# Score-factor broadcasts of the first pair by TensorE, setup weights in small tiles, and a finer order model, in a four-layer graph network

## The chip, the cores and the metric

The kernel runs on one core of a Trainium2 chip. The metric is the device time of the whole kernel in microseconds, the median of several executions. One further execution was taken under the hardware profiler; what is read from the profile comes from that one.

## The reference

There are 64 graphs of 256 nodes with 256 features, each with a 0/1 adjacency matrix of which about one entry in 64 is set. Four layers follow one another, each on the layer-normalised, rectified input, and each added to the running x:

```python
h = jnp.maximum(_layernorm(x, axis=-1), 0.0)
x = x + _L0_gnn_ref(h, adj, L0_gnn_W, L0_gnn_a_src, L0_gnn_a_dst)        # 4 heads of 64, slope 0.2, elu
h = jnp.maximum(_layernorm(x, axis=-1), 0.0)
x = x + _L1_gnn_ref(h, adj, L1_gnn_W, ...)                               # 4 heads of 64, slope 0.01, relu, residual, layer norm per head
h = jnp.maximum(_layernorm(x, axis=-1), 0.0)
x = x + _L2_gnn_ref(h, adj, L2_gnn_W, L2_gnn_a)                          # 1 head of 256, slope 0.2
h = jnp.maximum(_layernorm(x, axis=-1), 0.0)
x = x + _L3_gnn_ref(h, adj, L3_gnn_weight, L3_gnn_w_ih, ...)             # 3 rounds: adjacency sum, then a GRU cell
```

Layers 0 to 2 are graph attention. The score of an edge from i to j is a leaky ReLU of s_i + d_j, where s and d are products of the projected features with two vectors; a softmax over the neighbours weighs the projected features. In layer 3 a round is `m = h @ weight[i]`, `aggr = A^T m`, and a GRU cell with gates r, z and n on `aggr` and `h`.

## The kernel before, in words

The graphs go in 32 pairs. A pair's nodes are 4 blocks of 128 rows (C = 4), so its features are a tile `xt` of 128 x 4 x 256.

**An attention layer** (`heads_of`, or `layer2`). `norm` takes statistics on VectorE (L962, L963), the power -1/2 on GpSimd (L971, L972), and ScalarE writes the normalised, rectified `xn` (L980). `transposed` turns it by TensorE (L997) and ScalarE copies the banks into `ht`. `project` multiplies with the weights (L1019), in whose extra two columns per head stand the weights of s and d; ScalarE copies the result into `wh` (L1032, L1034). `factors` makes what the softmax needs. Since exp of a leaky ReLU of a sum is the larger of two products, each edge's weight is, up to a factor that the softmax divides out, the larger of f[0] and f[1] * cb, where `f` has one value per row j and head (L1072), and `cb` holds for every i the value exp((slope-1) * s_i), the same in all 128 partitions. To get `cb`, TensorE transposes the column of s to a row (L1053), ScalarE takes the exponential (L1060), ScalarE's DMA queue writes the row to memory (`rd`, L1065), and SP's queue reads it back for all partitions (`cb<-rd`, L1066; 1 MB for four heads, 256 KB for one). Then, for each head, `weights` makes `pt` by four VectorE instructions (L1087) and takes the minimum with `cap`, the mask made of the adjacency; `attend_head` multiplies `pt` with `wh` on TensorE (L1107), and VectorE divides by the sum.

**The mask.** SP loads the adjacency into the one `at` slot; ScalarE squares it (L1150, a check of the values), VectorE sums its rows (L1156), GpSimd casts it (`am`) and makes `cap_n` (L1164); TensorE turns that (L1177) and ScalarE copies it into `cap`.

**The GRU** (`gru`). Per round, TensorE does two aggregations (L1304), twelve gate groups (L1318; four 128-row products each with `ht`,`whh` or with `ag`,`wc`) and two row transposes (L1332); ScalarE takes the tanh, GpSimd one subtraction, and VectorE the rest.

**Setup.** The vectors of the scores are broadcast by ScalarE's queue into `ag` and `o` tiles; `score_column` multiplies them with the weights, reduces and copies the result into the weights' extra columns, all on VectorE. `input_gates` multiplies the three GRU weights with `w_ih` to `wc` (L925), from two tiles in the two `cb4_` slots, which are the same slots that hold a layer's `cb`.

**The order.** Nothing runs in the order in which it is written. Each `op(...)` only records an operation with its engine, a cost in nanoseconds, what it reads, writes and takes. `_Schedule.run` then plays all of them through once, at build time: an operation's due time follows backwards from the end of its pair, an engine that is idle takes the operation with the earliest due time whose inputs are done and whose buffers are free, and the instructions are emitted in that order. On each engine they run strictly in it. Buffers are slots of fixed number (`cb4_` 2, `at` 1, `pt` 3, `g` 9, `bank` 8, `xt` 5, and others), so a transfer also waits until its slot's last reader is done. All loads, broadcasts and stores but the small ones go through SP's queue, in order. Most VectorE, ScalarE and GpSimd instructions are issued by one helper, and so have one line, L807.

Of the kernel before, what the change touches and what calls it, by code (L numbers as in the profile page):

```python
# [517 lines left out]
SLOPES = (0.2, 0.01, 0.2)  # L518

# [18 lines left out]
class _Schedule:  # L538
# [8 lines left out]
    HOP = 300  # L547
    DMA_LATENCY = 2000
    DMA_RATE = 250.0
    STRETCH = 3.0  # L550

# [67 lines left out]

    def run(self):  # L620
        ops = self.ops
        for o in reversed(ops):
            late = self.end[o.group]
            for s in o.succs:
                if s.group == o.group or o.group not in self.end or o.group < 0:
                    late = min(late, s.due - self.STRETCH * s.cost - self.HOP)
            if o.nbytes:
                late -= self.DMA_LATENCY + o.nbytes / self.DMA_RATE
            o.due = late
# [17 lines left out]
        while True:  # L647
            for e in engines:
                if not idle[e]:
                    continue  # L650
                held = []
                while able[e]:
# [6 lines left out]
                    if all(len(self.free[c]) >= n for c, n in need.items()):  # L659
# [9 lines left out]
                        post(clock + o.cost, "free", o)  # L669
# [7 lines left out]
            while events and events[0][0] == clock:  # L677
                _, _, kind, o = heapq.heappop(events)
                if kind == "free":
                    idle[o.engine] = True  # L680
                    t = clock
                    if o.nbytes:
                        self.dma_free = max(self.dma_free, clock) + o.nbytes / self.DMA_RATE
                        t = self.dma_free + self.DMA_LATENCY
                        post(t, "done", o)
                    else:
                        post(t + self.HOP, "done", o)
                        for s in o.succs:
                            if s.engine == o.engine:
                                s.waits -= 1  # L690
                                if s.waits == 0:
                                    heapq.heappush(able[s.engine], (s.due, s.index))
                elif kind == "done":
                    done += 1
                    for s in o.succs:
                        if o.nbytes or s.engine != o.engine:
                            s.waits -= 1
                            if s.waits == 0:
                                heapq.heappush(able[s.engine], (s.due, s.index))
# [9 lines left out]
def _fast_path(  # L709
# [105 lines left out]
    def dma(engine, nbytes, emit, reads=(), writes=(), takes=()):  # L815
        op(engine, 450 if engine == "sp" else 120, emit, reads, writes, takes, nbytes)
# [4 lines left out]
    w3, wih = buf("cb4_", [P, L, DC, D]), buf("cb4_", [P, DC, G])  # L821
# [33 lines left out]
    for i in range(L):  # L855
        dma("sp", 1 << 18, lambda i=i: nc.sync.dma_start(
            w3.tile[:, i], w3t[i].rearrange("(c p) d -> p c d", p=P)), (), [(w3, i)])
    dma("sp", 3 << 18, lambda: nc.sync.dma_start(
        wih.tile, wih_t.rearrange("(c p) g -> p c g", p=P)), (), [wih])
# [4 lines left out]
    def score_column(B_we, w_ap, vec_buf, v_ap, dst, k, dc, s):  # L864
# [3 lines left out]
        vec(nc.vector.tensor_mul, 330, view, w_ap, v_ap,  # L868
            reads=[(B_we, (dc, "w")), vec_buf], writes=[tmp])
        col = lambda: cols.tile[:, dc, k : k + heads]  # L870
        vec(nc.vector.tensor_reduce, 330, col, view, AX.X, OP.add, reads=[tmp], writes=[(cols, (dc, k))])
        vec(nc.vector.tensor_copy, 80, dst, col, reads=[(cols, (dc, k))], writes=[(B_we, (dc, s))])
# [47 lines left out]
    def input_gates(i, dc, g0, g1):  # L920
        ps = bank()

        def mm():
            for ec in range(DC):
                nc.tensor.matmul(  # L925
                    ps.tile[:, : g1 - g0],
                    lhsT=w3.tile[:, i, ec, dc * P : (dc + 1) * P],
                    rhs=wih.tile[:, ec, g0:g1],
# [4 lines left out]
        op("pe", (g1 - g0) * 3.4, mm, [(w3, i), wih], [ps])  # L933
        vec(nc.scalar.copy, 150 + (g1 - g0), wc[:, i, dc, g0:g1], lambda: ps.tile[:, : g1 - g0],
            reads=[ps], writes=[(B_wc, (i, dc, g0))], engine="act")

    for i in range(L):
        for dc in range(DC):
            for g0 in (0, 512):
                input_gates(i, dc, g0, min(g0 + 512, G))  # L940
# [8 lines left out]
    op("dve", 300, gate_biases, [bi, bh], [B_bg])  # L949
# [5 lines left out]
    def norm(xt, cls):  # L955
# [19 lines left out]
        vec(nc.vector.scalar_tensor_tensor, 120, lambda: mv.tile[:, 3, :], lambda: mv.tile[:, 0, :], -1.0,  # L975
# [13 lines left out]
    def transposed(xn, cls):  # L989
        ht = buf(cls, [P, DC, S])  # L990

        def block(dc):
# [8 lines left out]
            op("pe", 470, emit, [xn], [ps], takes=[ht])  # L1001
# [7 lines left out]
    def project(ht, we, B_we, heads, width, shift):  # L1009
# [4 lines left out]
        def rows(c):  # L1014
# [12 lines left out]
            op("pe", 910, emit, [ht, B_we], [ps], takes=[wh])  # L1027
# [14 lines left out]
    def factors(wh, heads, width, slope, shift):  # L1042
# [6 lines left out]
        ps, row, rd = bank(), buf("row", [R, P]), buf("rd", [R, P])  # L1049
        cb = buf(f"cb{heads}_", [P, heads, C, P])  # L1050

        def emit_t():
            nc.tensor.transpose(  # L1053
                ps.tile[:R, :P], wh.tile.rearrange("p h c w -> p (h c) w")[:, :, width + 1], ident
            )

        op("pe", 150, emit_t, [wh], [ps])

        def emit_row():
            nc.scalar.activation(  # L1060
                row.tile, ps.tile[:R, :P], AF.Exp, scale=slope - 1.0, bias=-shift * (slope - 1.0)
            )

        op("act", 260, emit_row, [ps], [row])
        dma("act", 1 << 13, lambda: nc.scalar.dma_start(rd.tile, row.tile), [row], [rd])  # L1065
        dma("sp", heads << 18, lambda: nc.sync.dma_start(  # L1066
            cb.tile.rearrange("p h c n -> p (h c n)"),
            rd.tile.rearrange("(o r) n -> o (r n)", o=1).to_broadcast([P, R * P]),
        ), [rd], [cb])

        def exps(k, a):
            op("act", 250, lambda: nc.scalar.activation(  # L1072
# [8 lines left out]
    def weights(cap, f, cb, h):  # L1081
# [11 lines left out]
        for b in range(2):  # L1093
            for jc in range(2):
                op("dve", 440, lambda b=b, jc=jc: emit(b, jc), [cb, f], [(pt, (b, jc))])
# [16 lines left out]
    def attend_head(o, o_view, pt, wh, h):  # L1112
# [7 lines left out]
        op("pe", 980, emit, [pt, wh], [ps], takes=[o])  # L1120
        rs = buf("rs", [P, C])
        view = lambda: ps.tile[:, : C * w].rearrange("p (c w) -> p c w", c=C)
        vec(nc.vector.reciprocal, 190, lambda: rs.tile, lambda: view()[:, :, E], reads=[ps], writes=[rs])
# [344 lines left out]
```

## Time and profile before

| | |
|---|---|
| median of 3 runs | 3286.79 us (3286.14 to 3287.27) |
| profiled execution | 3288.5 us, its span 3286.6 us |
| TensorE busy | 3184.5 us, 97% of the span |
| VectorE | 2368.8 us, 72% |
| ScalarE | 1453.9 us, 44% |
| GpSimd | 1103.6 us, 34% |
| moved by DMA | 134.02 MB, 41 GB/s |

In the profile's lines PE is TensorE (PEld its weight loads), DVE is VectorE, ACT is ScalarE, POOL is GpSimd and SP is SyncE; DVEq, ACTq and SPq are the engines' queues. A line names the source line, the engine, the operation, the output and input by the program's names, the tile shapes and how many instructions. In a timeline the first two numbers are the start and the length in us, and a bracket at the end gives the idle time before the instruction and what ended it. PEclk is the granted TensorE clock in tenths of full speed.

### The profile page before, as it was taken

Reading aid. Unit: us, or ns where it says so; the run is one execution under the profiler, and the core shown is the slowest. Engines: PE = TensorE matmul, PEld = TensorE weight load, DVE = VectorE, ACT = ScalarE, POOL = GpSimd, SP = SyncE. Lnnn points to the kernel's source line nnn. Section 1 sums busy time; section 2 is a strip of 40 time slices with the busy share of each in tenths; the row PEclk is TensorE's granted clock in tenths of the full one; section 3 lists DMA queues with packets and bytes.
Section 4 is the critical chain, followed back from the end, with each engine's and each line's share of the span. In section 5 each row is a group of like instructions: output and inputs, shape, how many; then the busy total and the mean of one; then the engine's idle time right before and its main releaser. Section 6 shows DMA issues by size and latency. Waiting matters only on the chain.

```text
span 3286.6 us, 49515 instructions
## 1 busy us (share of the span) xinstructions
PE 3184.5 (97%) x19094; PEld 1890.3 (58%) x19094; DVE 2368.8 (72%) x4977; ACT 1453.9 (44%) x2829; POOL 1103.6 (34%) x1096
## 2 busy tenths in 40 slices
PE   6499999999999999999999999999999999999998
PEld 4355555655565565565555555655565565565554
DVE  6947777777777777777777777777777777776752
ACT  4244444544444444444544444544444444444432
POOL 2423332343432334332424432343432334332330
PEclk8799999999999999999999999999999999999999
DMA  4101110111110111011101110111111111011000
GB/s 137 43 21 39 39 43 30 49 38 41 46 47 32 36 43 49 33 44 41 43 30 56 40 43 30 49 37 41 48 38 41 36 43 49 33 36 36 30 10 14
DMA packets 73012, 134.02 MB, mean 41 GB/s; under 512 B 7872, under 2 KB 59840, under 8 KB 64576
## 3 DMA queue, kind: packets, MB, share of 16 engines
q1 hardware_dynamic: 68688, 129.38, 11.3%
q8 instruction: 153, 2.51, 0.3%
q10 hardware_dynamic: 4080, 1.39, 0.2%
q14 instruction: 91, 0.75, 0.1%
HBM read 113.38 MB, written 17.37 MB: 40 GB/s over the span
## 4 chain that ended last, share of the span: by engine, by line
PE 87%; DVE 4%; POOL 4%; issue 1%; ACT 1%; DVEq 0%; POOLq 0%; ACTq 0%
PE bank L1318 56%; PE bank L1107 11%; PE bank L1019 9%; PE bank L1304 5%; PE bank L997 3%; PE bank L1332 2%; POOL mean L1240 1%; DVE o L807 1%; POOL g L807 1%; DVE g L807 1%; POOL o L807 1%; ACT g L807 0%; PE bank L1177 0%; PE bank L1053 0%; DVE hl L807 0%
## 5 line engine op out<-in xcount | busy, mean ns | idle before, releaser
L1318 PE MATMUL bank<-ag,wc 128*128 128x512 f32 x2304 | 1058.7, 597 | 0.0
L1318 PE MATMUL bank<-ht,whh 128*128 128x512 f32 x2304 | 1052.3, 594 | 0.0
L807 ACT ACTIVATE g<-bank,bg 128x512 f32<-128x512 f32 x576 | 395.3, 686 | 1001.3 <-PE bank L1318 995.5
L1318 PEld LDWEIGHTS bank<-ag,wc 128*128 128x128 f32 x2304 | 425.6, 190 | 493.0 <-issue 481.6
L1318 PEld LDWEIGHTS bank<-ht,whh 128*128 128x128 f32 x2304 | 421.0, 190 | 455.3 <-issue 442.6
L807 DVE SCALAR_TENSOR_TENSOR g<-g,g 128x512 f32<-128x512 f32 x384 | 285.7, 744 | 319.8 <-ACT g L807 316.4
L1087 DVE TENSOR_SCALAR pt<-cb,f 128x256 f32<-128x256 f32 x1152 | 399.5, 421 | 114.6 <-PE bank L1107 100.8
L807 POOL TENSOR_TENSOR g<-ht,g 128x512 f32<-128x512 f32 x192 | 321.0, 1688 | 418.3 <-ACT g L807 418.3
L1107 PE MATMUL bank<-wh,pt 128*64 128x65 f32 x9216 | 405.1, 244 | 48.7 <-DVE pt L807 48.4
L1107 PEld LDWEIGHTS bank<-wh,pt 128*64 128x64 f32 x9216 | 331.7, 140 | 186.3 <-issue 122.4
L807 DVE TENSOR_TENSOR pt<-pt,cap 128x1024 f32<-128x1024 f32 x288 | 373.6, 1327 | 3.3
L807 POOL TENSOR_TENSOR o<-o,bias_b 128x512 f32<-128x512 f32 x64 | 92.8, 1450 | 576.5 <-DVE o L807 363.8
L1304 PE MATMUL bank<-am_r,hl 128*128 128x256 f32 x1536 | 236.1, 301 | 5.8 <-DVE hl L807 5.4
L807 ACT ACTIVATE g<-g,bg 128x512 f32<-128x512 f32 x192 | 133.2, 716 | 228.7 <-DVE g L807 228.7
L980 ACT ACTIVATE xn<-xt,mv 128x256 f32<-128x256 f32 x384 | 205.2, 589 | 65.3 <-DVE mv L807 64.9
L971 POOL TENSOR_SCALAR mv<-mv 128x4 f32<-128x4 f32 x128 | 31.1, 243 | 595.3 <-DVE mv L963 553.2
L1304 PEld LDWEIGHTS bank<-am_r,hl 128*128 128x128 f32 x1536 | 196.8, 190 | 40.9 <-issue 24.6
L962 DVE BATCH_NORM_STATS2 st<-xt 128x6 f32<-128x256 f32 x512 | 208.2, 407 | 12.1 <-DMA xt<-in_x_dram 8.8
L807 ACT COPY ht<-bank 128x512 f32<-128x512 f32 x256 | 139.5, 590 | 120.3 <-PE bank L997 114.3
L807 DVE TENSOR_TENSOR g<-g,bank 128x512 f32<-128x512 f32 x192 | 127.6, 683 | 74.8 <-PE bank L1318 74.8
L807 DVE RECIPROCAL rs<-bank 128x4 f32<-128x4 f32 (+1 forms) x384 | 56.3, 164 | 162.4 <-PE bank L1107 162.2
L1034 ACT COPY wh<-bank 128x264 f32<-128x264 f32 (+1 forms) x256 | 96.2, 376 | 132.2 <-PE bank L1019 130.2
(91 smaller groups left out, 3522.4 us busy)
## 6 DMA issues: line engine op xcount, KB each, us to landing
cb<-rd SPq DMA_DIRECT2D x64, 1024.0 KB
xt<-in_x_dram SPq DMA_DIRECT2D x32, 512.0 KB
at<-in_adj_dram SPq DMA_DIRECT2D x32, 512.0 KB
out_dram<-xt SPq DMA_DIRECT2D x32, 512.0 KB
cb<-rd SPq DMA_DIRECT2D x32, 256.0 KB
rd<-row ACTq DMA_DIRECT2D x64, 8.0 KB
cb<-in_L_gnn_w_ih_dram SPq DMA_DIRECT2D x1, 768.0 KB
cb<-in_L_gnn_weight_dram SPq DMA_DIRECT2D x3, 256.0 KB
```

Source lines behind the costliest of these rows:

```text
L807: op(engine, cost, lambda: fn(*[a() if callable(a) else a for a in args], **kw), reads, writes)
L962: nc.vector.bn_stats(st.tile[:, c, :], xt.tile[:, c, :])
L980: op("act", 610, lambda: nc.scalar.activation(xn.tile[:, c, :], xt.tile[:, c, :], AF.Relu, bias=mv.tile[:, 3, c : c + 1], scale=mv.tile[:, ...
L997: nc.tensor.transpose(ps.tile[:, c * P : (c + 1) * P], xn.tile[:, c, dc * P : (dc + 1) * P], ident)
L1019: nc.tensor.matmul(ps.tile[:, : heads * W], lhsT=ht.tile[:, dc, c * P : (c + 1) * P], rhs=we[:, dc].rearrange("p h w -> p (h w)"), start=( ...
L1034: nc.scalar.copy(wh.tile[:, :, c, :], src)
L1087: nc.vector.tensor_scalar(pt.tile[:, b, jc, :].rearrange("p (i n) -> p i n", n=P), cb.tile[:, h, 2 * b : 2 * b + 2, :], f.tile[:, 1, h, c ...
L1107: nc.tensor.matmul(ps[q * Q : (q + 1) * Q], lhsT=pt.tile[:, b, jc, i0 : i0 + Q], rhs=wh.tile[:, h, 2 * b + jc, :w], start=(jc == 0), stop= ...
L1240: nc.gpsimd.tensor_tensor(var.tile, var.tile, nhalf[:, :R], op=OP.pow)
L1304: nc.tensor.matmul(ps.tile[:, b * N : (b + 1) * N], lhsT=hl.tile[:, k, 2 * b + sc, :], rhs=am.tile[:, 2 * b + sc, :], start=(k == 0 and sc ...
L1318: nc.tensor.matmul(ps.tile, lhsT=w[:, dc, g * P : (g + 1) * P], rhs=v.tile[:, dc, :], start=(first and dc == 0), stop=(last and dc == DC - 1),
L1332: nc.tensor.transpose(ps.tile[:, c * P : (c + 1) * P], ht.tile[:, j, c * P : (c + 1) * P], ident)
```

## The change

Three things are changed together.

1. *Broadcast by TensorE.* For the first pair (`SPREAD_PAIRS = 1`), `factors` no longer goes through memory. For each head, `spread` issues four matmuls whose stationary operand is the column of s, repeated 128 times, and whose moving operand is the identity; every row of the result is then the column as a row. ScalarE takes the exponential straight into `cb`. That is nine heads: four in layer 0, four in layer 1, one in layer 2. `cb` is now tracked by head, so a head's `pt` waits for its own part. All other pairs do as before.
2. *Small setup tiles.* The GRU weights and `w_ih` are loaded as six tiles of 128 x 2 x 256 in `g` slots instead of two large ones in `cb4_`; `input_gates` makes three groups of 256 columns instead of one of 512 and one of 256. The multiplications of `score_column` go to GpSimd.
3. *Order model.* The costs of many operations are set anew, the single hop of 300 ns becomes one for each engine, an engine is taken as free again a little before its result is there (`OVERLAP`), due times get a margin of 200 ns instead of the hop, and SP holds back while more than 2 us of transfers are queued in the model. `PACE` is the same number as before under a name. With it, the order of nearly all instructions changes.

```diff
-    HOP = 300
+    OVERLAP = {"pe": 0, "act": 90, "dve": 80, "pool": 0, "sp": 0}
+    HOP = {"pe": 250, "act": 120, "dve": 120, "pool": 150, "sp": 0}
     DMA_LATENCY = 2000
-    DMA_RATE = 250.0
+    DMA_RATE = 220.0
+    DMA_AHEAD = 2000
     STRETCH = 3.0
+    MARGIN = 200.0
...
-                    late = min(late, s.due - self.STRETCH * s.cost - self.HOP)
+                    late = min(late, s.due - self.STRETCH * s.cost - self.MARGIN)
...
+                if e == "sp" and self.dma_free > clock + self.DMA_AHEAD:
                     continue
...
-                        post(clock + o.cost, "free", o)
+                        post(clock + o.cost - self.OVERLAP[e], "free", o)
...
-    w3, wih = buf("cb4_", [P, L, DC, D]), buf("cb4_", [P, DC, G])
+    w3, wih = ([buf("g", [P, DC, D]) for _ in range(3)] for _ in range(2))
...
-        vec(nc.vector.tensor_mul, 330, view, w_ap, v_ap,
-            reads=[(B_we, (dc, "w")), vec_buf], writes=[tmp])
+        vec(nc.gpsimd.tensor_tensor, 700, view, w_ap, v_ap, op=OP.mult,
+            reads=[(B_we, (dc, "w")), vec_buf], writes=[tmp], engine="pool")
...
+        def spread(h):
+            ps = bank()
+            def emit():
+                for c in range(C):
+                    nc.tensor.matmul(
+                        ps.tile[:, c * P : (c + 1) * P],
+                        lhsT=wh.tile[:, h, c, width + 1 : width + 2].to_broadcast([P, P]),
+                        rhs=ident, start=True, stop=True,
+                    )
+            op("pe", 880, emit, [wh], [ps], takes=[cb])
+            op("act", 700, lambda: nc.scalar.activation(
+                cb.tile[:, h].rearrange("p c n -> p (c n)"), ps.tile, AF.Exp,
+                scale=slope - 1.0, bias=-shift * (slope - 1.0),
+            ), [ps], [(cb, h)])
+
+        if sched.group < SPREAD_PAIRS:
+            for h in range(heads):
+                spread(h)
+        else:
+            ps, row, rd = bank(), buf("row", [R, P]), buf("rd", [R, P])
...
-        vec(nc.vector.reciprocal, 190, lambda: rs.tile, lambda: view()[:, :, E], reads=[ps], writes=[rs])
+        vec(nc.vector.reciprocal, 175, lambda: rs.tile, lambda: view()[:, :, E], reads=[ps], writes=[rs])
...
-            op("pe", 920, emit, [hl, am], [ps], takes=[ag])
+            op("pe", 1060, emit, [hl, am], [ps], takes=[ag])
...
-                vec(nc.gpsimd.tensor_tensor, 1330, lambda: d.tile, lambda: ht.tile[:, j, :],
+                vec(nc.gpsimd.tensor_tensor, 1500, lambda: d.tile, lambda: ht.tile[:, j, :],
```

## The prediction

> **What bounds the kernel now.** I read the page first, busy shares and then the forty slices, to see whether one engine carries the span and where it does not.
>
> ```profile
> span 3286.6 us, 49515 instructions
> PE 3184.5 (97%) x19094; PEld 1890.3 (58%) x19094; DVE 2368.8 (72%) x4977; ACT 1453.9 (44%) x2829; POOL 1103.6 (34%) x1096
> ...
> PE   6499999999999999999999999999999999999998
> ...
> PEclk8799999999999999999999999999999999999999
> ```
>
> TensorE is the bound: 97% of the span, and all of its idle time (3286.6 - 3184.5 = 102 us) is in the first two or three slices and the last. Next, busy times by stretch (columns: length, then busy time and instructions of PE, PEld, DVE, ACT, POOL, then granted clock, DMA share, GB/s) say how much idle lies where:
>
> ```profile
> 0.00:169.00 169.00, 88.23 (x915) 69.72 (x915) 129.25 (x326) 57.03 (x123) 59.33 (x72) 0.81 0.26 87
> 169.00:191.00 22.00, 22.00 (x60) 11.40 (x61) 7.25 (x17) 9.76 (x17) 8.37 (x12) 0.93 0.08 25
> 191.00:3100.00 2909.00, 2902.15 (x17443) 1719.55 (x17442) 2148.55 (x4492) 1322.97 (x2580) 994.71 (x977) 1.00 0.12 40
> ...
> 3200.00:3286.60 86.60, 74.23 (x235) 37.18 (x233) 26.11 (x36) 24.60 (x38) 10.65 (x9) 0.97 0.04 14
> ```
>
> 80.8 us of idle stand before 169, 6.9 in the 2909 us of the middle, 12.4 in the last pair's lone GRU. So the time is "when does the first GRU start" plus TensorE's remaining work. The timeline around the ramp shows what holds the start:
>
> ```profile
> 15.01 0.47 SPq L858 DMA_DIRECT2D cb<-in_L_gnn_w_ih_dram  x1
> 26.74 0.34 ACTq L1065 DMA_DIRECT2D rd<-row  x1
> 44.68 0.59 PE L925 MATMUL bank<-cb,cb 128*128 128x256 f32 x2
> 45.31 0.82 SPq L1066 DMA_DIRECT2D cb<-rd  x2
> 49.81 3.97 DVE L1087 TENSOR_SCALAR pt<-cb,f 128x256 f32<-128x256 f32 x12 [2.14 <-DMA cb<-rd]
> 93.81 1.39 DVE L1087 TENSOR_SCALAR pt<-cb,f 128x256 f32<-128x256 f32 x4
> 127.93 4.41 PE L1107 MATMUL bank<-wh,pt 128*64 128x65 f32 x96 [20.91 <-DVE pt L807]
> 150.70 2.57 DVE L1087 TENSOR_SCALAR pt<-cb,f 128x256 f32<-128x256 f32 x4
> 168.97 2.08 PE L1304 MATMUL bank<-am_r,hl 128*128 128x256 f32 x8 [0.32 <-ACT ht L807]
> ```
>
> Pair 0's factor row is written out at 26.7, but its broadcast is issued only at 45.3: both cb slots hold setup weights until the last L925 matmul. The first weights (pt) come at 49.8, layer 1's at 93.8, layer 2's at 150.7, the first aggregation at 169.0. Between them VectorE is 92% busy (40.66 of 44.0, 30.01 of 34.6), partly with pairs 1 and 2.
>
> **What the skill says.** "DMA: Bandwidth & Descriptors", section "Anatomy of one DMA", gives a fit of about 2 us fixed plus bytes over 436 GB/s (for another issue path). Here the row's write takes 1.44 us from its issue (2019.93) to the broadcast's issue (2021.37), and 1 MB of broadcast 4.5 us (45.31 to 49.81): same order. "TensorE: Matmul & The Clock Gate", Part 1, says that an idle window throttles the array; the ramp shows it, a clock of 0.66 to 0.76 from 60 to 160. "SBUF — State Buffer", "Who interferes with whom", says that a VectorE operation can be blocked by GpSimd; four pt pieces take 1.38 us as a rule and 2.57 at 150.7, with GpSimd 15 of 20 us busy.
>
> **The change, part by part.** Three things: nine broadcasts by TensorE for pair 0; setup weights in g tiles, so that cb is free; a new order. I follow the new order of instructions on each engine with durations of the trace of before.
>
> *First weights of pair 0: 24.7 instead of 49.8.* The norm's last step now stands behind the gate biases, which wait for a bias load issued at 9.3: 12.4 (11.65 before). ACT then makes xn before it squares the adjacency: done 14.5; the square to 15.6, transposes to 15.7, two ht copies to 16.7. The score products moved to GpSimd: no row shows that operation at 128x256. Half of the 128x512 rows (1.40 to 1.69) is 0.70 to 0.85; the ratio 1.96 of "GPSIMD Engine Reference", 3.1, times VectorE's 0.42 is 0.82. I take 0.8: four from 9.8 end at 13.0; VectorE's last w0e copy comes at 17.2, behind the adjacency's degrees and the am_r cast. Projection 17.3 to 22.0 (4.7 as at 19.8), mask transposes to 22.6, ACT's mask copy to 23.7, f to 24.0. A broadcast is four fp32 matmuls of 128 columns, eight passes. No row shows it: four transposes take 0.44; scaling a gate pass (429 ns for 512 columns) gives 8 x 107 = 0.86; eight weight loads of 190 ns unhidden give 1.5. I take 0.9. Nine are 8.1 us, less three transposes (0.8); they cost nothing in the sum, since TensorE is idle more than half of this stretch; without that cover, 7.3 us. ACT's exp of 128x512 is about 0.65 (the g<-o row, 0.63): first cb at 24.7.
>
> *The chain of pair 0 from there*, before and (estimated) after:
>
> first pt, layer 0: 49.8 | 24.7
> last statistics of layer 0: 67.7 | 45.3
> first pt, layer 1: 93.8 | 59.4
> last statistics of layer 1: 130.6 | 96.3
> first pt, layer 2: 150.7 | 109.5
> first aggregation: 169.0 | 128.3
>
> Layer 0: 17.9 us before; the new order puts a degree reduction (1.2), two score reductions (1.5), two statistics of pair 2 (1.1) into it and takes three pt of pair 1 (1.05) out: 20.6. One attend stands behind three setup matmul groups (2.6 us), which wait for the last weight loads: about 3.4 MB after 15.7; before, as much was issued from 15.0 and had landed by 29.2, so by 31; used from 33.6, hidden. To layer 1: the norm's GpSimd step, xn 2.2, TensorE behind five setup groups until 50.3, transposes 1.1, two more groups, projection 3.8, 0.5, a group, first broadcast and exp 1.6: 59.4. VectorE waits in between (53.2) for the third adjacency, which lands only after the one slot is read (47.6 + 4.5); pair 1's broadcast stands behind it on SP's queue. Layer 1 itself: as before, 36.9, with VectorE on pair 1's weights as filler. To layer 2: 13.2 instead of 20.1, without the DMA round trip (row 0.3, 1.4, 4.5) and with less filler. The last part: 18.8 against 18.3.
>
> *The sum.* First aggregation 40.7 us earlier. TensorE's groups ahead of it are the same in both orders but for four attends (24 against 20, layer 1 of pair 1) at 1.04: +4.2 behind it. These four wait for VectorE, which must first do pair 2's ELU and statistics: +3. The tail's order is the same for the last 85 us: 0. Later rounds: window below, 0. Span 3286.6 - 40.7 + 4.2 + 3 = 3253.1; the profiled execution took 3288.5 (1.9 around its span), 1.7 above the median of 3286.8, so 3255 there and **3253** in the median, 1.0% faster.
>
> **Rivals.**
>
> *Tighter rounds eat it: slower.* The planner's hop falls from 300 to 120 (150, 250). Look at layer 1 in a middle round (transpose of factors, the last minima, first attend):
>
> ```profile
> 2019.33 0.27 PE L1053 MATMUL bank<-ident,wh 128*16 128x128 f32 x1
> 2033.49 2.36 DVE L807 TENSOR_TENSOR pt<-pt,cap 128x1024 f32<-128x1024 f32 x2
> 2038.18 1.15 PE L1107 MATMUL bank<-wh,pt 128*64 128x65 f32 x32
> ```
>
> The first minimum ends near 2034.8, 3.4 us ahead of the attend. In the new order the attend follows the transpose after eight gates (13.7), two transposes (0.9), two aggregations (2.1), two row transposes (0.9): 17.6 us, not 18.9; VectorE starts pt at 10.8 as before, but an addition (0.7) stands ahead of the first minimum: 16.8 to 17.0. Slack 0.6. If VectorE is L late there, 31 rounds cost 31 x (L - 0.6); at L = 1.7 the gain is gone. For it: pt blocks did take 4.69 instead of 3.96 at 2074. Against: those 0.7 are inside or near the slack, other places (layer 2: 9.9 us for about 8.5) are no tighter than now. At L = 2.2, 3303.
>
> *Half the head start is lost.* VectorE is 92% busy in the ramp and follows one written order; a late adjacency or GpSimd's doubled load there (mask work, products, layer-norm) delays pair 0. With the first aggregation at 145: 3270.
>
> *More is gained.* TensorE idles less, so the clock is throttled less, and pair 0 gets VectorE sooner: 115, thus 3240.
>
> *The broadcasts were hidden anyway:* then the first pt would not have waited 2.14 us for a transfer, issued 0.6 after the slots came free; the round trip bounds only 5 to 7 us per layer, but cb's slots bound 19. I give it nothing apart.
>
> **Chances.** The forecast 0.62; half lost 0.18; more gained 0.08; tight rounds 0.12, of which 0.09 ends above +0.2% and 0.03 within. 0.2% (6.6 us) is about what three runs can tell, since they lie within 1.1 us. Faster 0.88, same 0.03, slower 0.09. The range, 3234 to 3279, takes in both lesser cases, the broadcast's and products' bounds (5 us on the chain, once each) and a loss of 0.8 us per round; it leaves out the slower case and the ends.
>
> **What would show it.** Right: first pt near 25, no wait for cb's DMA there, first aggregation near 128, about 40 us idle before it, 5 to 12 in the middle. Wrong: attends of layers 0 and 1 with waits for pt in every round; VectorE waiting for adjacency loads beyond 55; first aggregation past 145; a broadcast over 1.5 us.

## The result, and the profile after

The changed kernel takes 3321.07 us (median; 3320.47 to 3321.44) against 3287.03 us of the kernel before beside it (3286.14 to 3287.68). The ratio is 1.0104, with a 95% interval of 1.0086 to 1.0121: slower by about 34 us, where 34 us of gain were forecast, and 42 us beyond the end of the range (3279).

The page of the changed kernel, span, busy shares and the slices of TensorE and its clock:

```profile
span 3319.6 us, 49764 instructions
PE 3200.4 (96%) x19187; PEld 1891.6 (57%) x19187; DVE 2365.3 (71%) x4965; ACT 1449.0 (44%) x2841; POOL 1171.7 (35%) x1108
...
PE   7699999999999999999999999999999999999998
...
PEclk9899999999999999999999999999999999999999
```

The ramp at the left did become shorter. The loss is not to be seen in slices of tenths; the busy times by stretch show it (columns as in the prediction: length, then busy time of PE, PEld, DVE, ACT and POOL, then clock, DMA share, GB/s):

```profile
0.00:135.65 135.65, 87.72 (x879) 73.00 (x880) 104.43 (x271) 58.16 (x131) 48.27 (x71) 0.88 0.29 91
135.65:200.00 64.35, 59.82 (x308) 33.66 (x309) 46.03 (x74) 27.64 (x49) 28.84 (x27) 0.97 0.03 9
200.00:3100.00 2900.00, 2850.37 (x17074) 1674.95 (x17073) 2110.88 (x4423) 1286.67 (x2526) 1049.18 (x971) 1.00 0.12 40
```

TensorE now idles 47.9 us ahead of the first aggregation (80.8 before). But from 200 to 3100 it idles 49.6 us; before, the same stretch had 6.9. In the middle the order repeats from pair to pair, and the start of layer 1's projection comes every 100.45 us there in the mean; before, it was 98.66 over a cycle of three pairs. This mean is called the period below. The whole balance, from the two profiled executions: the first aggregation is 33.3 us earlier (168.97 to 135.65); what follows it takes 3183.9 in place of 3117.6 us, 66.3 more. Of these, 50 are idle time (71.3 against 21.3) and 16.3 are busy time, 4.2 of it the four attends that were moved behind the first aggregation. The sum is +33, as measured.

The timeline around the ramp, TensorE and VectorE, with the first weights of layers 0, 1 and 2 and the first aggregation:

```profile
24.80 5.48 DVE L1118 TENSOR_SCALAR pt<-cb,f 128x256 f32<-128x256 f32 x12
54.94 1.22 DVE L1187 TENSOR_REDUCE rs<-at 128x4 f32<-128x1024 int32 x1 [3.17 <-DMA at<-in_adj_dram]
62.51 1.71 DVE L1118 TENSOR_SCALAR pt<-cb,f 128x256 f32<-128x256 f32 x5 [2.59 <-ACT cb L1072]
106.72 2.80 PE L1005 MATMUL bank<-ident,xn 128*128 128x128 f32 x8 [14.64 <-ACT xn L988]
116.54 1.06 PE L1065 MATMUL bank<-ident,wh 128*128 128x128 f32 x8
118.80 1.38 DVE L1118 TENSOR_SCALAR pt<-cb,f 128x256 f32<-128x256 f32 x4 [3.56 <-PE bank L1138]
135.65 2.08 PE L1335 MATMUL bank<-am_r,hl 128*128 128x256 f32 x8 [0.32 <-ACT ht L814]
```

The first weights wait for no transfer any more and come where they were forecast. Layer 1 of the first pair then runs late.

What TensorE waits for from 200 to 3100, in the answer on waits (total, times, longest):

```profile
PE bank L1027 <- DVE hl L814: 18.7, 28, 0.7
PE bank L1363 <- DVE ht L814: 18.0, 32, 0.8
PE bank L1138 <- ACT ht L814: 12.8, 14, 0.9
```

Three waits, together 49.5 us and so nearly all of the 49.6, two of them about once per pair and the third with every second pair: L1363 are the row transposes of a new hidden state, which wait for VectorE's `ht`; L1027 is layer 0's projection, which needs a bank that VectorE's `hl` subtraction has yet to read; L1138 is an attend (the product of `pt` with `wh`) soon behind two groups of transposes, likewise for a bank. Layer 1's first attend, where the prediction put its rival, does not wait.

Here is one such place of the changed kernel, between the second and the third round of a pair's GRU: TensorE, then VectorE, then GpSimd.

```profile
2067.09 0.60 PE L1005 MATMUL bank<-ident,xn 128*128 128x128 f32 x4
...
2068.53 0.63 PE L1363 MATMUL bank<-ident,ht 128*128 128x128 f32 x4
2068.99 1.95 PE L1027 MATMUL bank<-w0e,ht 128*128 128x264 f32 x8
2071.41 0.63 PE L1363 MATMUL bank<-ident,ht 128*128 128x128 f32 x4 [0.48 <-DVE ht L814]
2073.61 1.16 PE L1027 MATMUL bank<-w0e,ht 128*128 128x264 f32 x4 [0.67 <-DVE hl L814]
...
2067.69 0.69 DVE L814 SCALAR_TENSOR_TENSOR ht<-g,g 128x512 f32<-128x512 f32 x1
2068.37 1.69 DVE L814 SCALAR_TENSOR_TENSOR g<-g,g 128x512 f32<-128x512 f32 x1
2069.98 0.68 DVE L814 TENSOR_TENSOR o<-o,mean 128x512 f32<-128x512 f32 x1
2070.59 0.68 DVE L814 SCALAR_TENSOR_TENSOR ht<-g,g 128x512 f32<-128x512 f32 x1
2071.19 1.76 DVE L1282 TENSOR_TENSOR xt<-xt,o 128x512 f32<-128x512 f32 x1
2072.87 1.28 DVE L814 TENSOR_TENSOR hl<-bank,hl 128x512 fp32r<-128x512 f32 x2
...
2068.02 1.49 POOL L814 TENSOR_TENSOR o<-o,beta_b 128x512 f32<-128x512 f32 x1
2070.74 1.65 POOL L814 TENSOR_TENSOR o<-o,gamma_b 128x512 f32<-128x512 f32 x1 [1.23 <-DVE o L814]
2072.48 1.60 POOL L814 TENSOR_TENSOR o<-o,beta_b 128x512 f32<-128x512 f32 x1
```

Two VectorE rows last 1.69 and 1.76 us where their kind takes 0.68. Each began 0.35 and 0.45 us after a GpSimd operation did, and each ends about 0.55 us after that one's end (2070.06 after 2069.51; 2072.95 after 2072.39). The first delays the second half of `ht`, for which the transposes wait; the second delays `hl`, for whose bank the projection waits. The subtraction `hl<-bank,hl`, one of whose operands is in PSUM, ran beside GpSimd's last operation at its usual length. The Trainium skill states this in "SBUF — State Buffer": a VectorE instruction with two SBUF inputs contends with a GpSimd instruction that reads SBUF ("Who interferes with whom"), and the one that issues second is blocked altogether until the first has finished ("Summary: rules for kernel authors"). These rows agree with it; one kind of GpSimd operation, further below, does not.

The kernel before has the same place with the same two kinds of operations, VectorE and then GpSimd:

```profile
2057.09 0.69 DVE L807 SCALAR_TENSOR_TENSOR ht<-g,g 128x512 f32<-128x512 f32 x1
2058.31 0.68 DVE L807 SCALAR_TENSOR_TENSOR g<-g,g 128x512 f32<-128x512 f32 x1
2059.03 0.69 DVE L807 SCALAR_TENSOR_TENSOR ht<-g,g 128x512 f32<-128x512 f32 x1
2059.64 1.76 DVE L807 TENSOR_TENSOR o<-o,mean 128x512 f32<-128x512 f32 x1
2061.32 0.68 DVE L807 TENSOR_TENSOR hl<-bank,hl 128x512 fp32r<-128x512 f32 x1
2062.56 1.74 DVE L1251 TENSOR_TENSOR xt<-xt,o 128x512 f32<-128x512 f32 x1 [0.57 <-POOL o L807]
...
2059.25 1.60 POOL L807 TENSOR_TENSOR o<-o,gamma_b 128x512 f32<-128x512 f32 x1
```

There operations are held for which nobody on TensorE waits yet. The order of VectorE differs as well: the first `xt<-xt,o`, which takes GpSimd's result and is held in both kernels, stands behind a subtraction `hl<-bank,hl` here and ahead of it in the changed kernel. VectorE's busy time is nearly the same in both kernels (2368.8 and 2365.3 us). In the means of each kind of row, the minimum `pt<-pt,cap` takes 1327 ns before and 1214 after, the GRU's `g<-g,g` 744 and 819, its `ht<-g,g` 702 and 732: a part of what VectorE loses to GpSimd has moved from operations with slack to those that TensorE waits for.

### The profile page after: what moved, and what is told of

Its sections match the earlier page's. It is cut to its first block, busy times and chain, and to the rows that moved or that the text cites. A ratio compares the mean times of both kernels' runs of the same rounds, so it can differ in the third digit from the quotient of the medians.

```text
span 3319.6 us, 49764 instructions
## 1 busy us (share of the span) xinstructions
PE 3200.4 (96%) x19187; PEld 1891.6 (57%) x19187; DVE 2365.3 (71%) x4965; ACT 1449.0 (44%) x2841; POOL 1171.7 (35%) x1108
## 4 chain that ended last, share of the span: by engine, by line
PE 81%; DVE 13%; POOL 3%; ACT 2%; issue 1%; DMA 0%; ACTq 0%; DVEq 0%; POOLq 0%
PE bank L1349 52%; PE bank L1138 10%; PE bank L1027 8%; PE bank L1335 5%; DVE g L814 4%; PE bank L1005 2%; POOL g L814 2%; DVE pt L1118 2%; DVE o L814 2%; PE bank L1363 2%; ACT g L814 2%; DVE ht L814 2%; DVE xt L1282 1%; DVE mean L814 1%; DVE hl L814 1%
## 5 line engine op out<-in xcount | busy, mean ns | idle before, releaser
L814 DVE SCALAR_TENSOR_TENSOR g<-g,g 128x512 f32<-128x512 f32 x384 | 313.4, 819 | 466.2 <-ACT g L814 448.0
L814 POOL TENSOR_TENSOR g<-ht,g 128x512 f32<-128x512 f32 x192 | 342.1, 1794 | 414.1 <-ACT g L814 414.1
L1138 PE MATMUL bank<-wh,pt 128*64 128x65 f32 x9216 | 399.9, 243 | 26.9 <-ACT ht L814 14.4
L1118 DVE TENSOR_SCALAR pt<-cb,f 128x256 f32<-128x256 f32 x1152 | 405.1, 421 | 22.8 <-DMA cb<-rd 14.7
L1138 PEld LDWEIGHTS bank<-wh,pt 128*64 128x64 f32 x9216 | 327.8, 139 | 155.1 <-issue 93.6
L814 DVE TENSOR_TENSOR pt<-pt,cap 128x1024 f32<-128x1024 f32 x288 | 341.6, 1214 | 1.1
L814 POOL TENSOR_TENSOR o<-o,bias_b 128x512 f32<-128x512 f32 x64 | 105.1, 1642 | 563.2 <-DVE o L814 538.5
L814 ACT COPY ag<-bank 128x512 f32<-128x512 f32 x192 | 112.5, 586 | 144.0 <-PE bank L1335 143.9
L980 POOL TENSOR_TENSOR mv<-mv,nhalf 128x4 f32<-128x4 f32 x128 | 149.7, 1169 | 10.7
```

The lines of the kernel that those rows point to most:

```text
L814: op(engine, cost, lambda: fn(*[a() if callable(a) else a for a in args], **kw), reads, writes)
L980: nc.gpsimd.tensor_tensor(mv.tile[:, 2, :], mv.tile[:, 2, :], nhalf[:, :C], op=OP.pow)
L1118: nc.vector.tensor_scalar(pt.tile[:, b, jc, :].rearrange("p (i n) -> p i n", n=P), cb.tile[:, h, 2 * b : 2 * b + 2, :], f.tile[:, 1, h, c ...
L1138: nc.tensor.matmul(ps[q * Q : (q + 1) * Q], lhsT=pt.tile[:, b, jc, i0 : i0 + Q], rhs=wh.tile[:, h, 2 * b + jc, :w], start=(jc == 0), stop= ...
```

## The experiments

Two theories stood against each other first: that the new planner's order costs every pair something and the setup half gains, or that the loss comes with the setup half itself or with starting earlier.

**The two halves apart.** The planner's class and its estimated costs were exchanged, nothing else; the costs of the setup's own operations stayed with the setup. In the changed kernel, back to those of before (the same in the other direction for the second run):

```diff
-    OVERLAP = {"pe": 0, "act": 90, "dve": 80, "pool": 0, "sp": 0}
-    HOP = {"pe": 250, "act": 120, "dve": 120, "pool": 150, "sp": 0}
+    HOP = 300
...
-    MARGIN = 200.0
...
-            vec(nc.gpsimd.tensor_tensor, 1500, lambda: o.tile[:, hs], lambda: o.tile[:, hs],
+            vec(nc.gpsimd.tensor_tensor, 1300, lambda: o.tile[:, hs], lambda: o.tile[:, hs],
```

> The changed kernel with the planner of before (its class and its estimated costs), so with the broadcasts by TensorE, the small setup tiles and GpSimd's products alone. In the middle its written order on TensorE is that of before (the same cycle of three pairs). Theory (the new planner's order costs every pair; the setup half of the change gains): the period is 98.7 us per pair again instead of 100.5, idle of TensorE from 200 to 3100 back under 10 us, first aggregation between 128 and 145, time 3250 to 3265. Rival (the loss comes with the setup half or with starting earlier, whatever the order): the period stays at 100.5 and the time stays within 10 us of 3321.

> The kernel before with the new planner alone (its class and its estimated costs): setup in large tiles and all broadcasts through memory as before. Theory: the middle has the changed kernel's order and its period of 100.5 us, TensorE idles over 45 us from 200 to 3100, and the time is the 3287 of before plus about 1.8 us for each of 29 pairs, 3330 to 3350 if the ramp is like that of before. Rival: no steady loss without the setup half, 3277 to 3297.

The first took 3259.93 us (ratio to before 0.9923, 0.9907 to 0.9940), the second 3362.55 (1.0233, 1.0216 to 1.0250). In the first the period is 98.65, the first aggregation at 133.93, and the idle time from 200 to 3100 is 7.3 us. In the second the period is 100.45 and that idle time 52.1. So the steady loss goes with the planner, whatever the setup. The second was slower than expected; its ramp is longer, too: first aggregation at 181.1, not 169.0. The setup half gains 26 us under the old planner and 41 under the new; the planner's half costs 76 with the old setup and 61 with the new.

TensorE's waits from 200 to 3100 in the changed kernel with the old planner, to be compared with the three above:

```profile
PE bank L1330 <- DVE hl L809: 6.0, 10, 0.6
PE bank L1022 <- DVE o L809: 0.7, 1, 0.7
PE bank L1022 <- DVE hl L809: 0.3, 1, 0.3
```

**Which half of the planner.** Its class and its costs were exchanged one at a time. (The class has one change more than the list above names: an operation that follows another on its own engine, TensorE excepted, counts as ready only a hop after that one's result, where it had been ready at once.)

> The changed kernel with the planner's class of before (one hop of 300 for all engines, no overlap, no look at the DMA queue, margin 300), but the new estimated costs. It tells apart which half of the new planner makes the tight order. If the hops of 120 do it: period back to 98.7 to 99.2, time 3250 to 3275. If the costs do it (GRU and mask operations priced differently): period 100 or more, time above 3300. Its order in the middle is neither that of before nor of the changed kernel (one cycle per pair, factor transpose ahead of the row transposes), so a third outcome between is open.

> The changed kernel with the new planner's class (short hops, overlap, look at the DMA queue) but the estimated costs of before. Its order at the boundary has a gate between the row transposes and the aggregations. If the short hops make the tight order: period 99.5 or more, time above 3290. If the costs do: period under 99, time 3255 to 3275. With both old 98.7 and with old hops and new costs 99.45 were measured, so I lean to the costs carrying about half: 99.5, 3290 to 3310.

3305.54 us (1.0058, 1.0041 to 1.0074) with the old class, 3293.20 (1.0018, 1.0011 to 1.0026) with the old costs; the periods, once the order has settled, are 99.45 and 99.59. Each of the two alone already writes an order that costs 0.8 to 0.9 us per pair, and together they cost 1.8. From 200 to 3100 TensorE idles 59.7 and 31.7 us. The places differ: with the old class the row transposes wait 34.0 us for `ht` (38 times), with the old costs the aggregation 19.4 us for `hl` (26 times). Neither half alone is the cause; which single constant matters was not tried.

**What the order suffers from.** GpSimd's operations for gamma and beta were shortened in the changed kernel, and in the one with the old planner as a control. The written order of TensorE, VectorE and ScalarE is untouched, and GpSimd's operations keep their places:

```diff
-            vec(nc.gpsimd.tensor_tensor, 1500, lambda: o.tile[:, hs], lambda: o.tile[:, hs],
-                lambda: each(gamma_b), op=OP.mult, reads=[B_gamma], writes=part, engine="pool")
...
+            vec(nc.gpsimd.tensor_tensor, 1500, lambda: o.tile[:, hs, :, 0:1], lambda: o.tile[:, hs, :, 0:1],
+                lambda: each(gamma_b)[:, :, :, 0:1], op=OP.mult, reads=[B_gamma], writes=part, engine="pool")
...
```

> The changed kernel in its own written order on every engine, but GpSimd's two operations of layer 1's norm (times gamma, plus beta) treat one column of 64 only, so that they last some 0.2 us in place of 1.6; what they leave out of the output is the scaling by gamma and the shift by beta of the other 63. Theory (the row transposes wait because VectorE's last operations of the GRU round are held while GpSimd's gamma and beta run): the waits for ht and hl at that boundary vanish, 1.2 to 1.35 us per pair and a drain each, period 98.8 to 99.2, idle of TensorE from 200 to 3100 from 50 down to 10 to 20 (the attends' wait for a bank, 13, stays), time 3270 to 3290. Rival (VectorE's order alone is too tight, whether or not GpSimd runs): idle stays over 35 us, time above 3305.

> The same shortening of GpSimd's gamma and beta operations in the kernel with the broadcasts and small tiles but the planner of before. Control: its order has slack at the boundary, so its middle has nothing to win there: period 98.5 to 98.7, idle from 200 to 3100 still 5 to 8 us, time within 5 us of 3260 (a few us less by a shorter ramp). If the shortening helps every order alike, the time falls by 20 us or more.

Shortened, gamma and beta take 0.61 and 0.39 us in the mean (1.67 and 1.47 before that). The changed kernel fell to 3266.20 us (0.9938 of before, 0.9922 to 0.9955), a little below what was expected, its idle time from 200 to 3100 from 49.6 to 14.7 us, its period from 100.45 to 98.8; the waits for `ht` and `hl` went to 1.0 and none. The control fell as well, to 3241.72 (0.9866, 0.9849 to 0.9882), 18 us where at most 5 were expected: period 98.27 in place of 98.65, first aggregation 3.9 us earlier. So GpSimd's operations cost something in either order, and the expectation that the old one has nothing to win was wrong; but the new order pays 55 us for them and the old one 18.

This left two readings: VectorE is kept from starting while they run, or they merely deliver late to VectorE's queue, where `xt<-xt,o` then holds up what stands behind it. A power of constants over 8 columns has GpSimd busy as long as a 128x512 addition but reads and writes little:

```diff
-            vec(nc.gpsimd.tensor_tensor, 1500, lambda: o.tile[:, hs], lambda: o.tile[:, hs],
-                lambda: each(gamma_b), op=OP.mult, reads=[B_gamma], writes=part, engine="pool")
...
+            vec(nc.gpsimd.tensor_tensor, 1500, lambda: o.tile[:, hs, :, 0], lambda: ones[:, :R].rearrange("p (h c) -> p h c", h=2),
+                lambda: nhalf[:, :R].rearrange("p (h c) -> p h c", h=2), op=OP.pow, reads=[B_gamma], writes=part, engine="pool")
...
```

> The changed kernel in its own order, with GpSimd's gamma and beta operations each replaced by a power of constants over 8 columns (leaves out the scaling and the shift; puts ones in one column of 64). Such a power lasts 1.65 us on GpSimd in the trace, as long as what it replaces, but VectorE's operations run at 0.68 beside it. So what waits for GpSimd's data comes as late as in the changed kernel, and only the holding goes. If holding is the cause: the waits for ht and hl vanish as with the short operations, idle from 200 to 3100 10 to 20, period 98.7 to 99.1, time 3262 to 3285. If the lateness of GpSimd's result is the cause (VectorE's queue waits for it): idle stays over 35 and the time above 3305.

It took 3276.64 us (0.9969, 0.9958 to 0.9980), with a period of 99.13 and 20.6 us idle from 200 to 3100, both just above what holding alone was expected to leave and far from what lateness was. The same place of this kernel, TensorE, VectorE, GpSimd:

```profile
2040.78 0.63 PE L1363 MATMUL bank<-ident,ht 128*128 128x128 f32 x4
2041.25 1.95 PE L1027 MATMUL bank<-w0e,ht 128*128 128x264 f32 x8
2043.03 0.64 PE L1363 MATMUL bank<-ident,ht 128*128 128x128 f32 x4
2043.51 1.95 PE L1027 MATMUL bank<-w0e,ht 128*128 128x264 f32 x8
...
2040.63 0.69 DVE L814 SCALAR_TENSOR_TENSOR g<-g,g 128x512 f32<-128x512 f32 x1
2041.84 0.68 DVE L814 SCALAR_TENSOR_TENSOR ht<-g,g 128x512 f32<-128x512 f32 x1
2042.44 0.69 DVE L1282 TENSOR_TENSOR xt<-xt,o 128x512 f32<-128x512 f32 x1
2044.80 0.69 DVE L814 TENSOR_TENSOR hl<-bank,hl 128x512 fp32r<-128x512 f32 x1 [1.07 <-ACT hl L1320]
2045.78 0.69 DVE L1282 TENSOR_TENSOR xt<-xt,o 128x512 f32<-128x512 f32 x1 [0.29 <-POOL o L814]
...
2040.28 5.46 POOL L814 TENSOR_TENSOR o<-ones,nhalf 128x8 f32<-128x8 f32 x3
```

GpSimd is busy throughout, VectorE's operations beside it take 0.68 or 0.69, and neither the transposes nor the projection wait. VectorE does now wait for GpSimd's result, 38.3 us in all at `xt<-xt,o` (6.4 in the changed kernel), and that costs TensorE little. So it is the holding: with that of gamma and beta gone and the lateness kept, 44 of the 55 us come back. VectorE as a whole is busy 68.6 us less than in the changed kernel (2296.7 us). The remaining 10 us are in part a new wait of 5.8 us in all, at gates for ScalarE. The attends' wait for a bank stays in both runs (13.7 and 13.8 us), so GpSimd's gamma and beta are not its cause.

The two runs also say something of TensorE's additional busy time. In the same order, with 57 fewer waits of the two kinds in each, TensorE is busy 8.2 us less with the powers and 14.5 less with the short operations (3192.2 and 3185.9 against 3200.4). As an estimate, a wait costs 0.14 to 0.25 us of busy time besides. That is near what two groups in a row overlap (a projection group of the kernel before, at 2059.62, lasts 1.06 us, and the transposes behind it start after 0.90), but that the lost overlap is the reason was not shown.

**What the broadcasts and the tiles are worth.** One constant back, under each planner:

```diff
-SPREAD_PAIRS = 1
+SPREAD_PAIRS = 0
```

> The changed kernel with pair 0's factors broadcast through memory like all others (SPREAD_PAIRS = 0); small tiles and new planner stay. Theory: same period of 100.5 us; the first aggregation is later by three round trips less three broadcasts, about 4.5 us each, so near 149, and the time near 3334 (3326 to 3342). If the cb slots alone had been what held the ramp, the broadcasts by TensorE are worth under 3 us and the time is 3318 to 3324.

> Small setup tiles and GpSimd's products with the planner of before, and all broadcasts through memory. It divides the 26 us of gain between broadcasts and tiles. Theory from the pair with the new planner (3344 without the broadcasts, 3321 with them): broadcasts worth about 20, time 3276 to 3284, first aggregation past 155. Rival (free cb slots did it, the broadcasts are worth one round trip per layer): 3262 to 3270.

3344.30 us (1.0176, 1.0159 to 1.0193) with the new planner and 3277.91 (0.9974, 0.9964 to 0.9984) with the old: the broadcasts by TensorE are worth 23 and 18 us, the small tiles with GpSimd's products the remaining 8 of the 26 under the old planner. The first aggregation comes at 166.9 and 161.9, far beyond what the three round trips counted in the expectation would give. In the first of these runs the cb transfer of layer 0 is issued at 27.45, and the first weights come at 32.39, 7.6 us later than with the broadcasts (24.80); those of layer 1 come 17.4 us later (79.96 against 62.51) and those of layer 2 27.5 (146.35 against 118.80). While a transfer is under way, VectorE goes on with pair 1, and pair 0 must then wait for it: at layer 1's first weights VectorE does not wait for the transfer, it is busy. How the delay divides between the transfers and VectorE's other work was not taken apart. The first weights of the three layers in that run:

```profile
32.39 4.00 DVE L1118 TENSOR_SCALAR pt<-cb,f 128x256 f32<-128x256 f32 x12 [2.44 <-DMA cb<-rd]
79.96 4.61 DVE L1118 TENSOR_SCALAR pt<-cb,f 128x256 f32<-128x256 f32 x12
146.35 4.20 DVE L1118 TENSOR_SCALAR pt<-cb,f 128x256 f32<-128x256 f32 x4
```

> Broadcasts by TensorE for the first two pairs, small tiles, planner of before. Nine more broadcasts of 0.9 us and nine more exps; the ramp waits for VectorE, not for pair 1's transfers, so within 4 us of 3260 if they fall into TensorE's idle time, up to 8 us more if behind the first aggregation.

3260.04 us (0.9915, 0.9899 to 0.9932), the same as with one pair: the first aggregation comes later, at 140.7, but with 98 us of TensorE's work ahead of it, not 86.

**Towards a better version.** The gamma and beta operations were moved to VectorE, nothing left out:

```diff
-            vec(nc.gpsimd.tensor_tensor, 1500, lambda: o.tile[:, hs], lambda: o.tile[:, hs],
-                lambda: each(gamma_b), op=OP.mult, reads=[B_gamma], writes=part, engine="pool")
+            vec(nc.vector.tensor_tensor, 700, lambda: o.tile[:, hs], lambda: o.tile[:, hs],
+                lambda: each(gamma_b), op=OP.mult, reads=[B_gamma], writes=part)
```

> Broadcasts, small tiles and the planner of before, with the two operations (times gamma, plus beta) moved from GpSimd to VectorE. A try at a better version: GpSimd's 6.4 us per pair that hold VectorE go, VectorE gets four operations of 0.68 more (2.7 us per pair, and is busy 71% of the time). If what held VectorE was worth as much as the shortened control showed (3242) the time is 3240 to 3258; if VectorE's longer queue at the GRU boundary costs as much, it is 3260 or more.

> The same with beta alone on VectorE and gamma still on GpSimd: half of each effect. 3245 to 3262 if fewer holds help, over 3262 if the order that the planner then writes is tighter.

> The changed kernel, new planner, with gamma and beta on VectorE, nothing left out. The written order changes too. Theory: the boundary's stalls were VectorE held by GpSimd, so the period falls from 100.45 to 98.6 to 99.4 and the time to 3265 to 3290. Rival (the new planner writes orders without slack anyway): period above 99.8, time above 3300.

> The changed kernel and its planner with bias, gamma and beta all on VectorE, nothing left out. Against gamma and beta alone (3233, period 97.9) two operations of GpSimd (1.45 us) less hold VectorE and it gets two of 0.68 more. If VectorE's length starts to count: 3233 to 3250. If holds still cost: 3222 to 3233.

Under the old planner 3248.53 us for both (0.9880, 0.9863 to 0.9896) and 3255.34 for beta alone (0.9905, 0.9888 to 0.9921). Under the new planner **3233.19 us** (0.9834, 0.9818 to 0.9851): 55 us faster than the kernel before beside it (3288.01), 88 faster than the changed one, and 32 below the lowest time that was expected. The stretches of that kernel:

```profile
0.00:128.02 128.02, 88.72 (x880) 73.18 (x880) 99.92 (x265) 56.34 (x128) 44.63 (x69) 0.89 0.30 92
...
200.00:3100.00 2900.00, 2894.44 (x17560) 1715.04 (x17559) 2192.40 (x4666) 1310.08 (x2579) 832.90 (x874) 1.00 0.12 40
```

Its period is 97.9, its idle time from 200 to 3100 5.6 us, and its first aggregation comes at 128.0. VectorE is busy 17 us more than in the changed kernel (2382.3), though it has 128 operations more (at 0.73 and 0.68 us, 90 us together): the difference is about what the powers had spared it in holds. Of the 91 us by which the profiled span is shorter than the changed kernel's, 62 are idle time and 29 TensorE's busy time. Not all of this can be put down to holds, since the planner wrote a new order for the kernel. With the same edit the new planner is 15 us ahead of the old one, where without it it was 61 behind. With bias moved too it is 3250.40 us (0.9894, 0.9877 to 0.9910), at the upper end of what was expected if VectorE's length starts to count. But TensorE idles only 3.3 us from 200 to 3100 there, and yet the period is 98.6 in most of the middle. TensorE's busy time per pair differs between orders that hardly wait, from 97.9 to 98.6. What makes that difference was not settled.

## Why the prediction was wrong, point by point

**The bound** was read rightly: TensorE carries the span, and the time is the start of the first aggregation plus what TensorE has left. Two readings beside it were a little off, without effect on the sum: of the two windows named for VectorE the first is 92% busy, the second 87%, and the clock between 60 and 160 goes down to 0.64, not 0.66.

**First weights of pair 0: 24.7.** Measured 24.80. A broadcast was priced at 0.9. It leaves eight records; layer 2's single one took 1.06 (at 116.54), four in a row took 3.84 (layer 0) and 3.73 (layer 1), so 0.93 to 0.96 each. That term holds. The close agreement of the whole is in part luck: the norm's last step ended at 13.6, not 12.4, and `xn` at 15.8, not 14.5, which did not show because the projection had been expected at 17.3 for another reason, VectorE's copies of the weights.

**The chain from there: 128.3.** Measured 135.65. The steps between layers held (14.0 against 14.1 to layer 1, 13.3 against 13.2 to layer 2). Layer 0 took about 3 us more: its twelve `pt` lasted 5.48 where they had taken 3.97, beside GpSimd's mask cast (1.04 us at 25.16) and two of the moved products (0.68 and 0.69 us from 26.16), and the foreseen wait for the third adjacency came, 3.17 us at 54.94, off the path. Layer 1, priced "as before, 36.9", took 43.0. VectorE did more in that stretch than in the one of before, 85 instructions and 39.6 us in place of 65 and 32.1 (the changed kernel, then the kernel before; length, busy time and instructions of VectorE, then clock, DMA share, GB/s):

```profile
62.50:105.50 43.00, 39.59 (x85) 0.80 0.11 38
93.80:130.60 36.80, 32.05 (x65) 0.69 0.08 30
```

So work of other pairs that the new order puts there was left out of the price. Holding by gamma and beta is a smaller part: from layer 1's first weights to the transposes behind it there pass 44.2 us, and 43.2 with the powers in their place (62.08 to 105.26). The head start was thus 33 us, not 40.7.

**Four attends behind the first aggregation: +4.2, and +3 of waiting.** Ahead of the first aggregation stand 544 matmuls of attends in place of 672, which is four attends of 32, and TensorE idles 4.5 us from 135.65 to 200, where before it had no idle time between 169 and 200. Both held in size. With the old planner the whole sum comes out in kind: first aggregation 35.0 us earlier, profiled span 28.6 us shorter, so 6.4 us are lost behind it where 7.2 were allowed.

**Later rounds: 0.** This is the step that failed, by about 59 us: what follows the first aggregation takes 66.3 us more, where the sum allowed 7.2. The 0 was reached from a single window, layer 1's first attend, and the sentence that other places are no tighter than now. The places where TensorE takes up what VectorE has just finished at the GRU's round were not examined. On TensorE itself the one shown above is hardly tighter: some 2.2 us of work stand between the two row transposes in either order. What moved is the work of the other two engines beside it. VectorE's second `ht` starts some 0.45 us later, counted from the first transpose of `xn` behind the last gates: 2.49 us after it where nothing is held (the run with the powers), 2.04 in the kernel before; and `xt<-xt,o` stands ahead of `hl`. In the run with the powers TensorE still does not wait at this place, so this alone costs little. GpSimd's work moved more: counted from the same transpose, GpSimd's gamma starts 2.3 us later in the kernel before, when VectorE is nearly done with `ht` (2059.25 after 2056.99), and in the changed kernel beta starts after 0.9 us (2068.02 after 2067.09), with VectorE in the midst of it. The prediction followed TensorE and VectorE through its window, but not GpSimd against VectorE, and priced an addition there at its free length, 0.7, though the prediction itself cited a held piece (at 150.7), and the trace of before had `xt<-xt,o` at 1202 ns and `o<-o,mean` at 1189 in the mean.

**The rival "tighter rounds eat it: slower"** is what happened in kind: VectorE late in every round by a steady amount, at 1.8 us per pair well past the 1.1 or so (34 us over 31 rounds) from which the gain is gone. Its place was wrong and its cause (an addition ahead of a minimum) too, and it had been given a chance of 0.12. "Half the head start lost" did not come: 135.65 is short of 145.

**The tail: 0.** From 3100 to the end TensorE idles 17.1 us, 14.5 before; nothing of weight.

## What to carry to other kernels

When a change rewrites an order, its middle must be read at every place where TensorE takes up what VectorE has just finished, not at one; a loss of 1.8 us that repeats thirty times outweighs 33 us won once. An operation's length in such a place is not its best length: beside a GpSimd addition of 128x512, VectorE operations with two SBUF operands ended only about 0.55 us after it (1.76 us in place of 0.68), and an order planned without that can put the hold where it is paid for. Where the bound engine waits for VectorE, count what GpSimd runs at that moment, and try giving its work to VectorE: here four operations of 0.7 us more per pair on VectorE, with the order planned anew, made the kernel 88 us faster.

## What the runs showed of the hardware that was not expected

The hold does not follow GpSimd's busy time: a power over 8 columns has GpSimd busy for 1.64 us or more, and VectorE's two-operand rows ran at 0.68 to 0.69 beside it, while additions of 128x512 of the same length held them to 1.7. The rule cited above would have such a power, which reads SBUF too, block them until it ends; in the run with the powers no row is held in this way, and the measurement decides. A held VectorE row ended 0.55 us after the GpSimd operation, near the length of the row itself. A plain `pt<-cb,f` row (one SBUF tensor and a column per partition) was held as well: three of them at 94.76, beside GpSimd's beta, took 3.05 us, where three at 49.14 without the broadcasts took 1.05. And by the estimate above a wait of TensorE costs 0.14 to 0.25 us of busy time in addition to the idle time that the profile counts.
